# A graph attention's keys and values set up in a hand-written order, with rows and values placed through DRAM

## The chip, the cores and the metric

The kernel runs on one core of a Trainium2 chip. A core has a matrix engine (TensorE, PE in the profile), three engines for elementwise work (VectorE or DVE, ScalarE or ACT, GpSimd or POOL), and a queue engine (SyncE, SP) that issues transfers between DRAM and the on-chip memory. Each engine works through its own instructions in order; they meet only at semaphores. The metric is the device time of one execution in microseconds. Before the change it was 3151.98 us, the median of three runs (3148.44 to 3156.79).

## The reference

Two layers run one after the other on `x` of shape (4, 1024, 512), with a condition vector per batch. The first is a graph attention over 20 neighbours in two directions, the second a conditioned transformer block.

```python
row_zero = v.sum(-1) == 0
vcq = concatenate([v, where(row_zero[..., None], 0.0, q[:, None, :])], -1)
self_feat = vcq @ W_self.T + b_self
output = self_feat
for d in range(2):                       # A: the mask, or its transpose
    kv = self_feat[:, :20]
    qh = (self_feat @ Wq[d].T + bq[d])   # 16 heads of 32
    kh = (kv @ Wk[d].T + bk[d])
    aff = einsum('bnhd,bmhd->bnhm', qh, kh) / sqrt(32)
    w = softmax(where(A.sum(-1) > 0, aff, NEG) + (A @ w_bias + b_bias))
    out_t = einsum('bnhm,bmf->bnhf', w, kv)
    output += einsum('bnhf,hgf->bnhg', out_t, Wout[d]) + bout[d]
x = v + relu(output)
# then: layer norm with scale and shift from the condition, attention with
# 16 heads of 64, gated residual, and an MLP of 2048 with gelu, gated residual
```

Only the first 20 rows of a batch are keys and values in the graph attention. So 80 rows (4 batches of 20) settle everything that depends on keys and values, and that is computed once, ahead of the 32 row blocks.

## The kernel before, in words

The kernel has a set-up (lines 149 to 341), a loop over 32 blocks of 128 rows for the graph attention (lines 841 to 889), the transformer attention, and the MLP. The change touches the set-up and the start of the loop.

The set-up loads the 80 neighbour rows beside their conditions (`vcq`, lines 157 to 160), the two halves of the self weights (`wx`, `wq_in`, line 163), the biases as rows (`rows`, line 172), and per direction d the key, query and output weights (line 177). All loads are issued by SP. Then it computes, in the order of the code:

- the biases transposed to columns (`vecs`, line 187), and the condition transposed (`condT`, `scT`, line 197);
- the condition's share of the self feature, four rows (`pq`, line 203), which one matrix product per batch spreads to all 128 partitions (`pr`, line 210) and a copy puts into `qrB`;
- the self features of the 80 rows, transposed (`pf`, lines 223 to 239): 32 small products, 80 columns wide;
- per direction: keys (`pk`, line 272), values (`pvr`, line 283), the keys laid out block by block (`kbd`, line 300), and the query weights and biases folded into them (`pw`, `pb`, lines 313 and 322), copied into `kp` and `qbB` by ScalarE and VectorE in turn (`evac`, lines 78 to 83);
- the values placed so that each head's rows meet only their own 32 columns (`vb`): matrix products with a zero-one matrix `spr` (line 334) and a multiplication with a mask `own` (line 341). GpSimd builds both (lines 243 to 263).

A planner in the framework orders these instructions on each engine. From line 608 on the order is by hand: each engine issues what the code issues, in the code's order.

The loop runs steps s from -4 to 33. Step s handles several blocks at different stages: it loads block s + 4, transposes block s + 3, multiplies block s + 2 by the self weights, and so on. `g_load(i)` (line 613) issues the 128 rows of block i (`xs`, seven buffers) and two pieces of its adjacency (`a`, two buffers) on SP. An adjacency buffer comes free when GpSimd has converted it (`af`, line 675). Step -4 loads blocks 0 to 4:

```python
        for s in range(-4, NTA + 2):
            if s == -4:
                for i in range(5):
                    g_load(i)
            else:
                do(g_load, s + 4)
```

Steps -3 to 0 load blocks 1 to 4 a second time, and what later reads block 1 reads that second copy (36 loads of `xs` are in the profile for 32 blocks). The buffers of the loop lie where the set-up's tiles lay, so each waits until the tiles below it have been read for the last time.

Of the kernel before, what the change touches and what calls it, by code (L numbers as in the profile page):

```python
# [12 lines left out]
F32 = mybir.dt.float32  # L13
# [6 lines left out]
P = 128  # L20
# [21 lines left out]
def cond_block_kernel(  # L42
# [42 lines left out]

    cst = ctx.enter_context(tc.tile_pool(name="cst", bufs=1))
# [41 lines left out]
    x1d = [tc.dram_tile([P, F], F32, name=f"x1d{i}") for i in range(NTA)]  # L128
    x2d = [tc.dram_tile([P, F], F32, name=f"x2d{i}") for i in range(NTA)]


    with ExitStack() as gctx:
# [15 lines left out]

        with ExitStack() as sctx:
            sp = sctx.enter_context(tc.tile_pool(name="sp", bufs=1))  # L150
            sps = sctx.enter_context(tc.tile_pool(name="sps", bufs=4, space=PSUM))
            mps = sctx.enter_context(tc.tile_pool(name="mps", bufs=2, space=PSUM))
# [3 lines left out]
            nc.sync.dma_start(cnd, cond)  # L156
            for b in range(B):
                q = slice(b * NG, (b + 1) * NG)
                nc.sync.dma_start(vcq[q, :F], x[b * S : b * S + NG, :])
                nc.sync.dma_start(vcq[q, F:], cond[b : b + 1, :].broadcast_to([NG, F]))  # L160
            wq_in = sp.tile([P, FC, F], F32, name="wq_in")
            for t, src in ((wx, w_selfT[:F]), (wq_in, w_selfT[F:])):
                nc.sync.dma_start(t, src.rearrange("(c p) f -> p c f", p=P))
# [9 lines left out]
            ws = []  # L173
            for d in range(2):
                for src in (gwkT, gwq, gwoT):
                    t = sp.tile([P, FC, F], F32, name=f"w{d}", tag=f"w{len(ws)}")
                    nc.sync.dma_start(t, src[d].rearrange("(c p) f -> p c f", p=P))
                    ws.append(t)
            gboB = sp.tile([KV, 2, F], F32, name="gboB")
            for d in range(2):  # L180
                nc.sync.dma_start(gboB[:, d, :], gbo[d : d + 1, :].broadcast_to([KV, F]))
            nc.sync.dma_start(bsB, row(b_self).broadcast_to([P, F]))
# [3 lines left out]
            pv = sps.tile([P, F], F32, name="pv", tag="s")  # L186
            nc.tensor.transpose(pv[:, :N_VEC], rows, ident[:N_VEC, :N_VEC])
            nc.vector.tensor_copy(vecs, pv[:, :N_VEC])

            silu = sp.tile([B, F], F32, name="silu")  # L190
            nc.scalar.activation(silu, cnd, AF.Silu)
            condT = sp.tile([P, FC, B], F32, name="condT")
            nc.vector.memset(scT, 0.0)
            for t, src in ((condT, cnd), (scT[:, :, :B], silu)):
                pc = sps.tile([P, FC, B], F32, name="pc", tag="s")
                for c in range(FC):
                    nc.tensor.transpose(pc[:, c, :], src[:, c * P : (c + 1) * P], ident[:B, :B])
                nc.vector.tensor_copy(t, pc)

# [7 lines left out]
            nc.vector.tensor_copy(qrows, pq[:B])  # L207
            for b in range(B):
                pr = sps.tile([P, F], F32, name="pr", tag="s")
                nc.tensor.matmul(pr, lhsT=one_hot(0, b), rhs=qrows, start=True, stop=True)  # L210
                evac(b, qrB[:, b, :], pr)


            nz = sp.tile([KV, 1], F32, name="nz")
            nc.vector.tensor_reduce(nz, vcq[:, :F], axis=AX.X, op=ALU.add)
            nc.vector.tensor_scalar(nz, nz, 0.0, None, ALU.not_equal)
            nc.vector.tensor_scalar(vcq[:, F:], vcq[:, F:], nz, None, ALU.mult)
            vcqT = sp.tile([P, 2 * FC, KV], F32, name="vcqT")
            for h in range(2):
                pt = sps.tile([P, FC, P], F32, name="pt", tag="s")  # L220
                for c in range(FC):
                    k = h * FC + c
                    nc.tensor.transpose(pt[:, c, :KV], vcq[:, k * P : (k + 1) * P], ident[:KV, :KV])
                evac(h, vcqT[:, h * FC : (h + 1) * FC, :], pt[:, :, :KV])
            sfT = sp.tile([P, FC, KV], F32, name="sfT")
            for c in range(FC):
                pf = sps.tile([P, F], F32, name="pf", tag="s")
                for k in range(2 * FC):
                    w = wx if k < FC else wq_in
                    nc.tensor.matmul(  # L230
                        pf[:, :KV],
                        lhsT=w[:, k % FC, c * P : (c + 1) * P],
                        rhs=vcqT[:, k, :],
                        start=(k == 0),
                        stop=(k == 2 * FC - 1),
                    )
                nc.vector.tensor_scalar(
                    sfT[:, c, :], pf[:, :KV], vecs[:, V_SELF + c : V_SELF + c + 1], None, ALU.add
                )


            spr = sp.tile([KV, B, 2, GH, 2, NG], F32, name="spr")
            nc.gpsimd.memset(spr, 0.0)
            for b in range(B):
                for d in range(2):
                    nc.gpsimd.tensor_copy(
                        spr[:, b, d, :, d, :],
                        ident[:KV, b * NG : (b + 1) * NG].unsqueeze(1).to_broadcast([KV, GH, NG]),
                    )
            own = sp.tile([P, KC0, GHC, GD], F32, name="own")  # L250
            nc.gpsimd.memset(own, 1.0)
            W2 = 2 * NG
            skip = P - (GHC - 1) * W2
            for at, sign in ((0, 1), (W2 - 1, -1)):
                nc.gpsimd.affine_select(
                    out=own,
                    in_=own,
                    compare_op=ALU.is_ge,
                    fill=0.0,
                    base=at,  # L260
                    pattern=[[sign * skip, KC0], [-sign * W2, GHC], [0, GD]],
                    channel_multiplier=sign,
                )

            vrow = []
            for d in range(2):
                wk, wq, wo = ws[3 * d : 3 * d + 3]

                pk = sps.tile([P, GCH, KV], F32, name="pk", tag="s")
                for c in range(GCH):  # L270
                    for k in range(FC):
                        nc.tensor.matmul(
                            pk[:, c, :],
                            lhsT=wk[:, k, c * P : (c + 1) * P],
                            rhs=sfT[:, k, :],
                            start=(k == 0),
                            stop=(k == FC - 1),
                        )


                po = sps.tile([P, F], F32, name="pvr", tag="s")
                for k in range(FC):
                    nc.tensor.matmul(
                        po[:KV], lhsT=sfT[:, k, :], rhs=wo[:, k, :], start=(k == 0), stop=(k == FC - 1)
                    )
                v = sp.tile([KV, F], F32, name="vrow", tag="vrow", bufs=2)
                nc.vector.tensor_tensor(v, po[:KV], gboB[:, d, :], ALU.add)
                vrow.append(v)
# [7 lines left out]
                kbd = sp.tile([P, GCH, B, GHC, NG], F32, name="kbd", tag="kbd", bufs=2)  # L296
                nc.gpsimd.memset(kbd, 0.0)
                for h in range(GHC):
                    q = slice(GD * h, GD * (h + 1))
                    nc.vector.tensor_copy(  # L300
                        kbd[q, :, :, h, :], kh[q].rearrange("p c (b m) -> p c b m", b=B)
                    )

                def placed(t, c):

                    return t.rearrange("p b (h d m) -> p b h d m", d=2, m=NG)[:, :, c * GHC : (c + 1) * GHC, d, :]


                for c in range(GCH):
                    flat = kbd[:, c].rearrange("p b h m -> p (b h m)")  # L310
                    for f in range(FC):
                        pw = sps.tile([P, B, GHC, NG], F32, name="pw", tag="s")
                        nc.tensor.matmul(
                            pw.rearrange("p b h m -> p (b h m)"),
                            lhsT=wq[:, c, f * P : (f + 1) * P],
# [4 lines left out]
                        evac(f, placed(kp[:, :, f, :], c), pw)  # L320
                    pb = sps.tile([P, B, GHC, NG], F32, name="pb", tag="s")
                    nc.tensor.matmul(
                        pb.rearrange("p b h m -> p (b h m)"),
                        lhsT=vecs[:, V_Q + d * FC + c : V_Q + d * FC + c + 1].to_broadcast([P, P]),
                        rhs=flat,
                        start=True,
                        stop=True,
                    )
                    evac(c, placed(qbB, c), pb)
            for b in range(B):  # L330
                pv2 = mps.tile([P, KC0, P], F32, name="pv2", tag="m")
                for k in range(KC0):
                    for d in range(2):
# [1213 lines left out]
```

## Time and profile before

| what | value |
|---|---|
| median of three runs | 3151.98 us |
| the profiled execution | 3151.38 us, span 3149.7 us |
| TensorE busy | 3087.7 us, 98% of the span |
| set-up, last product of line 334 | ends at 88.5 us |
| first transposes of the loop (block 0) | 89.47 us |
| transposes of block 1 | 90.83 us |
| DMA in the first 30 us | 8 weight tiles of 1 MB and the small loads |

The profile is of one execution. Times in it are microseconds from the start of the span. An engine's busy time is the time in which it executes instructions; register, semaphore and DMA-issuing instructions do not count. A line of the timeline gives the start, the duration, the engine (SPq is SP's queue), the source line, the operation, the tile written and the tiles read, and in brackets the idle time before it with what ended it. A line with x8 merges eight instructions. A line of the stretches gives the stretch, its length, the busy time of PE, weight loads, DVE, ACT and POOL with instruction counts, the clock granted to TensorE as a share of full speed, the DMA share and GB/s. A line of the waits names who waited for whom, the total, the number of waits and the longest.

### The profile page before, as it was taken

The page shows a single profiled execution, that of the slowest core. Times are in us where ns is not written, and L with a number is a line of the kernel's source. Part 1 is how long each engine was busy: PE and PEld are TensorE (multiplying, and loading weights), DVE is VectorE, ACT ScalarE, POOL GpSimd, SP SyncE. Part 2 cuts the span into 40 slices and gives each one's busy share as a digit, 9 for nine tenths or more (in the row PEclk, how much of TensorE's full clock was granted, in tenths as well). Part 3 has the DMA queues.
Part 4 walks back from the last instruction along what each step waited for, and adds up shares of the span by engine and source line. Part 5 has one row for each costly group of instructions (what it writes and reads, how often), then busy time and mean ns, then how long its engine had stood idle before and what let it go on. Part 6 is the DMA issues. An engine that isn't in the chain of part 4 may idle for free.

```text
span 3149.7 us, 41147 instructions
## 1 busy us (share of the span) xinstructions
PE 3087.7 (98%) x15211; PEld 1957.9 (62%) x15211; DVE 1996.0 (63%) x2793; ACT 1437.6 (46%) x2387; POOL 1203.0 (38%) x739
## 2 busy tenths in 40 slices
PE   8999999999999999999999999999989999999999
PEld 5666665554554555454555455455458888888888
DVE  2688867777787777778777778777764232223322
ACT  1344446555665555665555665556631221112211
POOL 1344436554554654454644454555522100111010
PEclk8999999999999999999999999999999999999999
DMA  4233317776777876777776777776861010101010
GB/s 166 71 97 105 106 48 177 181 170 150 194 169 175 196 172 153 192 170 177 196 168 156 187 174 178 184 176 150 195 172 65 30 36 32 41 14 40 27 41 14
DMA packets 272859, 405.40 MB, mean 129 GB/s; under 512 B 24660, under 2 KB 97424, under 8 KB 272660
## 3 DMA queue, kind: packets, MB, share of 16 engines
q1 hardware_dynamic: 272660, 402.78, 50.8%
q8 instruction: 121, 1.98, 0.3%
q14 instruction: 78, 0.64, 0.1%
HBM read 109.08 MB, written 25.17 MB: 43 GB/s over the span
## 4 chain that ended last, share of the span: by engine, by line
PE 85%; DVE 5%; ACT 3%; issue 2%; DMA 2%; SPq 1%; POOL 1%; POOLq 0%; DVEq 0%; ACTq 0%
PE q L467 16%; PE psc L1065 14%; PE pav L1027 13%; PE pout L1045 7%; PE mbd L467 5%; PE mbu L467 5%; PE mad L467 4%; PE mau L467 3%; PE pa L695 2%; PE mcd L467 2%; PE pf L655 2%; ACT w L1082 2%; PE mdd L467 2%; PE mdu L467 2%; PE mcu L467 2%
## 5 line engine op out<-in xcount | busy, mean ns | idle before, releaser
L1091 POOL TENSOR_SCALAR w<-w,sm 128x1024 f32<-128x1024 f32 x256 | 733.8, 2866 | 884.3 <-DVE sm L1087 884.1
L1082 ACT ACTIVATE w<-psc,mx 128x1024 f32<-128x1024 f32 x512 | 570.5, 1114 | 645.3 <-DVE mx L1076 644.5
L1100 DVE STREAM_TRANSPOSE wd<-w 128x1024 f32<-128x1024 f32 x512 | 633.8, 1238 | 134.8 <-ACT w L1089 115.1
L1076 DVE TENSOR_REDUCE mx<-psc 128x1 f32<-128x1024 f32 x512 | 599.5, 1211 | 102.5 <-PE psc L1065 99.8
L1065 PE MATMUL psc<-kT,qT 64*128 64x512 f32 x2048 | 531.3, 617 | 6.8 <-ACT w L1082 4.2
L1027 PE MATMUL pav<-wT,v 128*64 128x256 f32 x4096 | 475.1, 382 | 2.3 <-DMA wT<-wd 1.7
L1027 PEld LDWEIGHTS pav<-wT,v 128*64 128x64 f32 x4096 | 290.1, 137 | 225.3 <-issue 70.4
L1065 PEld LDWEIGHTS psc<-kT,qT 64*128 64x128 f32 x2048 | 204.2, 186 | 262.7 <-issue 158.0
L1089 ACT ACTIVATE w<-w,sm 128x1024 f32<-128x1024 f32 x256 | 291.0, 1137 | 0.0
L1045 PE MATMUL pout<-wout,oT 128*128 128x512 f32 x512 | 243.5, 609 | 5.8 <-DVE xr L1053 5.8
L449 POOL TENSOR_TENSOR tx<-hT 128x512 f32<-128x512 f32 x8 | 10.2, 1270 | 568.5 <-DVE hT L388 568.5
L467 PE MATMUL q<-hT,wqk 128*128 128x512 f32 (+1 forms) x396 | 183.1, 586 | 6.7 <-DVE q L481 6.7
L1045 PEld LDWEIGHTS pout<-wout,oT 128*128 128x128 f32 x512 | 92.9, 191 | 137.4 <-issue 118.0
L489 ACT COPY mbu<-mau 128x512 f32<-128x512 f32 x30 | 17.1, 570 | 291.7 <-PE mau L467 291.7
L695 PE MATMUL pa<-kp,sfT 128*128 128x320 f32 x512 | 143.5, 433 | 1.4 <-ACT sfT L670 1.4
L1053 DVE TENSOR_TENSOR xr<-pout,xr 128x512 f32<-128x512 f32 x128 | 85.5, 680 | 85.4 <-PE pout L1045 85.1
L467 PEld LDWEIGHTS q<-hT,wqk 128*128 128x128 f32 x396 | 73.1, 190 | 102.7 <-issue 99.1
L467 PE MATMUL q<-tx,ex 128*128 128x512 f32 (+1 forms) x264 | 126.6, 603 | 0.0
L695 PEld LDWEIGHTS pa<-kp,sfT 128*128 128x128 f32 x512 | 94.8, 190 | 38.2 <-ACT sfT L670 1.9
L655 PE MATMUL pf<-wx,xT 128*128 128x512 f32 x256 | 115.3, 593 | 0.3 <-DVE pf L637 0.3
L467 PE MATMUL mad<-w,hs 128*128 128x256 f32 x512 | 113.1, 379 | 0.0
L467 PEld LDWEIGHTS mad<-w,hs 128*128 128x128 f32 x512 | 97.3, 190 | 13.2
(303 smaller groups left out, 4364.8 us busy)
## 6 DMA issues: line engine op xcount, KB each, us to landing
wT<-wd SPq DMA_DIRECT2D x1024, 256.0 KB
wqk<-in_w_qkv SPq DMA_DIRECT2D x64, 256.0 KB
xs<-in_x SPq DMA_DIRECT2D x36, 256.0 KB
x1d<-xs SPq DMA_DIRECT2D x32, 256.0 KB
xl<-x1d SPq DMA_DIRECT2D x32, 256.0 KB
wv<-in_w_qkv SPq DMA_DIRECT2D x32, 256.0 KB
xr<-x1d SPq DMA_DIRECT2D x32, 256.0 KB
wout<-in_w_out SPq DMA_DIRECT2D x16, 512.0 KB
```

The source lines that it names most:

```text
L467: nc.tensor.matmul(t[:, q * width : (q + 1) * width], lhsT=lhs(which, q, k), rhs=rhs(which, q, k), start=(fresh and q == 0 and k == 0), st ...
L655: nc.tensor.matmul(pfs[i], lhsT=xT[i][:, c, :], rhs=wx[:, c, :], start=False, stop=(c == FC - 1), skip_group_check=True,)
L695: nc.tensor.matmul(pas[i][:, n, :HF], lhsT=sfT2[i][:, c, :], rhs=kp[:, b, c, n * HF : (n + 1) * HF], start=False, stop=(c == FC - 1), skip ...
L1027: nc.tensor.matmul(po[j * D : (j + 1) * D, :], lhsT=vt[b, g][:, m, p * P + j * D : p * P + (j + 1) * D], rhs=w[:, j, :, m, :], start=(m == 0),
L1045: nc.tensor.matmul(po, lhsT=oT[b, 2 * g + p][:, n * P : (n + 1) * P], rhs=wout[b, g][:, p, :], start=(p == 0), stop=(p == 1),)
L1053: nc.vector.tensor_tensor(t, po, t, ALU.add)
L1065: nc.tensor.matmul(sc[j][:, n * F : (n + 1) * F], lhsT=qT[b, gp][q, t * P : (t + 1) * P], rhs=kT[b, gp][q, n * F : (n + 1) * F], start=Tru ...
L1076: nc.vector.tensor_reduce(mx, sc, axis=AX.X, op=ALU.max, negate=True)
L1082: nc.scalar.activation(w, sc, AF.Exp, bias=mx, accum_out=sm)
L1089: nc.scalar.mul(w, w, sm)
L1091: nc.gpsimd.tensor_scalar(w, w, sm, None, ALU.mult)
L1100: nc.vector.transpose(wd[j][:, :, at, :], wn.pop((b, gp, t, j)).rearrange("p (m k) -> p m k", k=U))
```

## The change

- The order by hand begins at the top of the kernel, so it covers the set-up too.
- Until the first loads land, TensorE multiplies a cleared tile `warm` by itself, seven products of 512 columns.
- The neighbour rows and the condition are loaded on ScalarE's queue, the weights on SP's. The self weights' first half comes first, and per direction the order is key, output, query weights. A direction's row bias follows its weights.
- The buffers of `xs` and `a` move to a pool of their own, opened ahead of the set-up, and blocks 0 and 1 are loaded right behind the weights. Step -4 loads blocks 2 to 4. The second loads of blocks 1 to 4 stay.
- The self features are summed in one bank, first over the rows' half of the weights for all four column chunks, then over the condition's half, with the small transposes between. The bias rows are transposed after that.
- The four condition rows are written to DRAM and read back onto all partitions, in place of the products `pr`.
- The values are written to DRAM and read back head by head into a cleared `vb`: 36 small loads on SP (16 heads, two directions, four heads cut in two at a multiple of 128 rows). The products of line 334, `spr` and `own` are gone.
- The order of the rest is keys 0, values 0, keys 1, folding 0, values 1, folding 1. Half of the copies into `kbd` go to ScalarE. The set-up has seven PSUM banks for its tiles in place of four, and one for the busy work.

```diff
+    ctx.enter_context(tc.manual_schedule())
     cst = ctx.enter_context(tc.tile_pool(name="cst", bufs=1))
...
+    qrd = tc.dram_tile([B, F], F32, name="qrd")
+    vrd = [tc.dram_tile([KV, F], F32, name=f"vrd{d}") for d in range(2)]
...
+        lp = gctx.enter_context(tc.tile_pool(name="lp", bufs=1, reuse_waits="tile"))
+        def g_load(i):
+            xs[i] = lp.tile([P, F], F32, name="xs", tag="xs", bufs=7)
+            nc.sync.dma_start(xs[i], x[i * P : (i + 1) * P, :])
+            adjs[i] = lp.tile([P, 2, NG * NL], I32, name="a", tag="a", bufs=2)
+            for d in range(2):
+                nc.sync.dma_start(adjs[i][:, d, :], adj[d, i * P : (i + 1) * P, :])
...
-            sps = sctx.enter_context(tc.tile_pool(name="sps", bufs=4, space=PSUM))
-            mps = sctx.enter_context(tc.tile_pool(name="mps", bufs=2, space=PSUM))
+            sps = sctx.enter_context(tc.tile_pool(name="sps", bufs=7, space=PSUM))
+            wps = sctx.enter_context(tc.tile_pool(name="wps", bufs=1, space=PSUM))
...
+                nc.scalar.dma_start(vcq[b * NG : (b + 1) * NG, :F], x[b * S : b * S + NG, :])
+            nc.sync.dma_start(wx, w_selfT[:F].rearrange("(c p) f -> p c f", p=P))
+            nc.scalar.dma_start(cnd, cond)
+            for b in range(B):
+                nc.scalar.dma_start(
+                    vcq[b * NG : (b + 1) * NG, F:], cond[b : b + 1, :].broadcast_to([NG, F])
+                )
+            nc.sync.dma_start(wq_in, w_selfT[F:].rearrange("(c p) f -> p c f", p=P))
...
+                for k, src in ((0, gwkT), (2, gwoT), (1, gwq)):
+                    nc.sync.dma_start(ws[3 * d + k], src[d].rearrange("(c p) f -> p c f", p=P))
                 nc.sync.dma_start(gboB[:, d, :], gbo[d : d + 1, :].broadcast_to([KV, F]))
+            for i in range(2):
+                g_load(i)
...
+            warm = sp.tile([P, F], F32, name="warm")
+            nc.vector.memset(warm, 0.0)
+            for d in range(2):
+                nc.gpsimd.memset(kbds[d], 0.0)
+            nc.gpsimd.memset(vb, 0.0)
+            def warming(n):
+                t = wps.tile([P, F], F32, name="pwarm", tag="warm")
+                for _ in range(n):
+                    nc.tensor.matmul(t, lhsT=warm[:, :P], rhs=warm, start=True, stop=True)
+            warming(7)
...
+            neighbours(0)
+            nc.vector.tensor_scalar(vcq[:, F:], vcq[:, F:], nz, None, ALU.mult)
+            through_self(0)
+            neighbours(1)
...
+            through_self(1)
...
-                pr = sps.tile([P, F], F32, name="pr", tag="s")
-                nc.tensor.matmul(pr, lhsT=one_hot(0, b), rhs=qrows, start=True, stop=True)
-                evac(b, qrB[:, b, :], pr)
+            nc.scalar.copy(qrows, pq[:B])
+            nc.sync.dma_start(qrd, qrows)
+                nc.sync.dma_start(qrB[:, b, :], qrd[b : b + 1, :].broadcast_to([P, F]))
...
+                nc.vector.tensor_tensor(v, po[:KV], gboB[:, d, :], ALU.add)
+                nc.sync.dma_start(vrd[d], v)
+
+            def spread_values(d):
+                src = vrd[d].rearrange("(b m) f -> m b f", b=B)
+                for h in range(GH):
+                    q = (2 * h + d) * NG
+                    cuts = [q, *range((q // P + 1) * P, q + NG, P), q + NG]
+                    for a, z in zip(cuts, cuts[1:]):
+                        k, p = divmod(a, P)
+                        col = h * GD - k * 3 * GD
+                        nc.sync.dma_start(
+                            vb[p : p + z - a, :, k, col : col + GD],
+                            src[a - q : z - q, :, h * GD : (h + 1) * GD],
+                        )
...
+            keys(0)
+            values(0)
+            keys(1)
+            spread_values(0)
+            folded(0)
+            values(1)
+            spread_values(1)
+            folded(1)
...
-        ctx.enter_context(tc.manual_schedule())
...
-                for i in range(5):
+                for i in range(2, 5):
                     g_load(i)
```

## The prediction

> **What bounds the kernel now.** I read the page's head first, then the chain that ended last, then the opening by tens of microseconds, then its timeline, then the load queue's own waits.
>
> ```profile
> span 3149.7 us, 41147 instructions
> ...
> PE 3087.7 (98%) x15211; PEld 1957.9 (62%) x15211; DVE 1996.0 (63%) x2793; ACT 1437.6 (46%) x2387; POOL 1203.0 (38%) x739
> ...
> PE 85%; DVE 5%; ACT 3%; issue 2%; DMA 2%; SPq 1%; POOL 1%; POOLq 0%; DVEq 0%; ACTq 0%
> ```
>
> TensorE is busy 98% of the span and carries 85% of the chain. What shortens its opening shortens the kernel, as long as nothing late makes it wait. The opening, in the answer by stretches (its last columns: granted clock, DMA share, GB/s):
>
> ```profile
> 10.00:20.00 10.00, 7.07 (x17) 1.92 (x17) 0.57 (x3) 0.00 (x0) 3.43 (x4) 1.00 1.05 403
> 20.00:30.00 10.00, 9.23 (x27) 5.05 (x27) 2.55 (x4) 1.60 (x3) 0.00 (x0) 0.63 1.03 372
> 30.00:40.00 10.00, 10.00 (x49) 10.00 (x49) 0.90 (x3) 0.00 (x0) 0.00 (x0) 0.50 0.02 4
> 2340.00:2350.00 10.00, 4.23 (x7) 1.57 (x6) 8.11 (x21) 0.00 (x0) 0.00 (x0) 0.68 0.50 155
> ```
>
> From 22.5 to 46.4 us TensorE is busy but granted half its clock, while the loads are over by 30. The last line shows what a gap costs: TensorE idles 5.77 us there. The timeline:
>
> ```profile
> 12.94 0.33 PE L187 MATMUL pv<-ident,rows 60*128 60x60 f32 x1 [12.94 <-DMA rows<-in_b_mod]
> ...
> 14.13 6.06 PE L203 MATMUL pq<-wq_in,condT 128*4 128x512 f32 x8
> ...
> 20.96 5.67 PE L210 MATMUL pr<-qrows,ident 4*128 4x512 f32 x8 [0.77 <-DVE qrows L207]
> ...
> 27.88 2.00 PE L230 MATMUL pf<-vcqT,wx 128*128 128x80 f32 x8
> ...
> 61.68 3.69 PE L272 MATMUL pk<-sfT,w 128*128 128x80 f32 x32
> ...
> 79.42 9.10 PE L334 MATMUL pv<-vrow,spr 80*128 80x128 f32 x80
> ...
> 90.83 0.66 PE L649 MATMUL pt<-ident,xs 128*128 128x128 f32 x4
> ```
>
> TensorE starts at 12.94, when the bias rows land behind the weights. The pr and the 80-product pv go with the change, pq and pf should run faster. The last line, the transposes of row block 1, is my mark: everything after 90.83 is the same work in the same order, so its new time gives the result. The load queue:
>
> ```profile
> SPq L618 <- POOL af L675: 47.4, 4, 21.9
> ...
> 61.95 0.80 SPq L618 DMA_DIRECT2D a<-in_adj  x2
> 62.80 0.43 SPq L615 DMA_DIRECT2D xs<-in_x  x1
> 63.33 0.85 SPq L618 DMA_DIRECT2D a<-in_adj  x2
> ```
>
> Row blocks are loaded in order on SP and waiting there costs nothing today: what block 1 needs is issued at 65.65, 25 us early. That cover is what the change uses up.
>
> **The change part by part.** Every matrix product here is two TensorE instructions. A half of 512 columns takes 0.43 us at full clock, 0.86 at half (the pq row's spacing); an 80-column half 0.110 (32 from 61.84 to 65.38 on the chain) or 0.213 (64 from 27.9 to 41.5).
>
> *Keeping TensorE busy.* Seven products of zeros, 14 halves, start once VectorE has cleared their 512 columns, near 1.6. The clock came up 5.1 us after pq's dense halves began (spacing falls at about 19.2) and 3.8 us after work resumed at 2346.65. So they end between 1.6 + 3.8 + 9.6 x 0.43 = 9.5 and 10.2; if zeros do not count, at 1.6 + 12.0 = 13.6. I take 10.2. Loads: neighbour rows were used 1.5 us after issue and go first now; the two self weights need 2 MB at the 409 GB/s shown, 5.1 us, and land by 9. Nine loads on ScalarE's own queue at 0.33 us take 3 us of an engine idle until 22 today; its first copy is due at 10.7. GpSimd's clearings (2.3 us, and 2.2 for the values by half of the 4.36 us memset) end by 7 and are due at 27: nothing.
>
> A rule against the whole idea: the Trainium skill, TensorE: Matmul & The Clock Gate, "Why this matters for your kernels", asks for 4 us of continuous work and no more for full clock. Here TensorE was busy 15 us (27.9 to 42.8) in 80-column products and stayed at 0.50. By the page the self stage would run at full clock after the warm-up and the price below would be 0, not 2.5.
>
> *Self stage.* From 10.2: four transposes and ScalarE's copy 1.1 (0.5 + 0.43 + hand-over); 32 halves 3.5; four transposes, eight small ones for the condition, a copy: 1.6; 32 halves 3.5; biases 0.3; pq 3.4. That is 23.6. At half clock the second 32 cost 3.3 more and pq 1.7 more, 5.0. The 1.6 us of thin work in the middle may drop the clock: it fell at 22.5 after an interval with pq to 20.2 and four-row products behind it, yet stayed up through 80-column products mixed with dense ones (60 to 65). I take half of the range 0 to 5.0: 2.5, so 26.1.
>
> *Keys and values.* keys 3.5, values 3.4, keys 3.5, folding four times 2.69 (the chain's 2.15 + 0.54): 10.8; values 3.4. Call the end of those second values E: 26.1 + 24.6 = 50.7. The second folding ends at E + 10.8. The four-row spreading of the query rows (5.7 us) and the 80 spreading products (9.1 us) are gone from TensorE; the DRAM trips replacing them are on SP. VectorE's one add for the self stage (320 columns, 0.49 as kh) lies beside pq. Copies keep up: 0.43 and 0.49 us on two engines against 0.54 per fold. Then 0.95 idle and 1.4 to the mark, as in 88.51 to 90.83: E + 13.1 = 63.8 if block 1 is there.
>
> *What is late next.* SP now holds, in order: query rows out (about 26), four reads back, values 0 out, 18 small loads, values 1 out, 18 small loads, and only then blocks 2, 3, 4 and block 1 again (line 846 repeats it, and the transposes read the repeat). The first set (values 0 end at 33.0, the same steps as below) is through by about 44, before E. The second: VectorE's add and issue E + 1.35; the write lands about 1.9 later. No row shows a write to DRAM awaited; a small load took 1.2 (condition, 1.17 to 2.36), a loaded queue 3.0 (64.18 to 67.16); 1.9 is nearer the first because the queue is empty. Then 18 issues. Twenty-row loads of vcq are issued every 0.37 us, wb and bb every 0.64; four loads into interleaved columns of wm took 2.08, so interleaving forces no wait. I take 0.41: 7.4. SP is free at E + 10.6. Before, from the first a at 61.95, a of block 4 landed at 68.6 by the wait of its successor; block 1's rows, behind it in the queue, 0.8 later (256 KB at the 330 GB/s between the last two landings): 7.4 after 61.95, plus 0.8 for block 2's rows, now in front: 8.2. Unloaded bound: 4.55 + 1.2 = 5.8. So block 1 is there at E + 18.8, and TensorE waits 5.7 (2.6 at the best ends, 10 with 0.64).
>
> The Trainium skill, DMA: Bandwidth & Descriptors, "Specifications", wants 512 B per piece for line rate; these are 128 B. Priced as 512 B, an estimate, 1,440 pieces are 0.74 MB, 1.8 us at 409 GB/s, under the 7.4 of issuing, so its sum is mine; no row here shows 128-byte pieces.
>
> *The gap's clock.* After the 5.77 us gap the clock was back 3.8 us after resuming: 1.9 us lost. I add 1.9.
>
> **Sum:** 63.8 + 5.7 + 1.9 = 71.4 against 90.83: 19.4 us less. The profiled execution took 3151.4 (its span and 1.7 around it); 3132.0. The median of the three runs is 0.6 higher: 3132.6.
>
> **The rivals.**
> *No late block.* The small loads issue at 0.37 and block 1 lands unloaded; stall at most 2.6, no clock loss, and the self stage stays warm: E 48.2, mark 63.9, 26.9 less, 3125. For: DMA is idle then. Against: 65.65 to about 69.4 for the same load before.
> *The busy work has no effect.* Zeros do not raise the clock. Warm-up ends 13.6; the self stage costs 1.3 + 6.8 + 2.2 + 6.8 + 0.3 + 5.1; E is 60.7, mark 81.4, 9.4 less, 3143. For: the four-row products at 20.96 did not hold the clock, so not all work counts. Against: these use all 128 rows.
> *Slower: SP serialises the small loads.* If each waits for the one before (2.2 us), the first set, from 36.3, ends near 76, the second near 118, block 1 comes at 126, and with 1.9 of clock the mark is 37 us later: 3189. It decides from 1.2 us per load (36.3 + 36 x 1.17 + 2.25 + 8.2 + 1.9 = 90.8). Against: vcq's and wm's paces of 0.37 and 0.52 into one tile.
> *Dearer issue*, 0.64: 4.1 more, 3137, inside the main case's range.
>
> **How the numbers follow.** Main case with dearer issue 0.65, no late block 0.12, no effect 0.14, serialised 0.09. Measurement tells about 0.3% (9.5 us; the runs spread over 3148.4 to 3156.8). Faster: 0.65 + 0.12 + half of 0.14, less a few hundredths for dear issue with a cold self stage: 0.81; same 0.11; slower 0.08. Range: from 3124 (no late block) to 3146 (no effect, with a dearer issue's 4 us); the main case's own is 3127 to 3140.
>
> **What would show it.** The mark near 71; a TensorE wait of 3 to 10 us just before it, put down to the load of xs; the clock at 0.50 for a few microseconds after it; pw starting near 36 instead of 50.9; 36 small loads about 0.4 us apart on SP. I am wrong if the self stage's products take 0.21 us throughout, if the small loads lie over 1.2 us apart, or if the wait before the mark is absent.

## The result, and the profile after

The changed kernel takes 3132.76 us, the median of four runs (3130.72 to 3134.16), against 3150.21 us for the kernel before on the same chip (four runs, 3148.18 to 3156.79). The ratio is 0.9945, with a 95% interval from 0.9928 to 0.9961: 17.5 us less. The prediction was 3132.6. The profiled execution took 3134.16 us, its span 3132.4.

The head of the page of the changed kernel, and the line of its chain by engines:

```profile
span 3132.4 us, 41033 instructions
...
PE 3074.0 (98%) x15137; PEld 1939.2 (62%) x15137; DVE 1989.6 (64%) x2780; ACT 1440.3 (46%) x2391; POOL 1195.1 (38%) x728
...
PE 84%; DVE 5%; ACT 4%; DMA 2%; issue 2%; SPq 2%; POOL 1%; POOLq 0%; DVEq 0%; ACTq 0%
```

TensorE is still busy 98% of the span. It has 13.7 us less of busy time, and SP's queue holds 2% of the chain in place of 1%. Its timeline through the opening:

```profile
1.47 9.27 PE L215 MATMUL pwarm<-warm 128*128 128x512 f32 x14 [1.47 <-DVE warm L205]
10.57 0.44 PE L230 MATMUL pt<-ident,vcq 80*128 80x80 f32 x4
11.53 3.80 PE L237 MATMUL pf<-vcqT,wx 128*128 128x80 f32 x32 [0.52 <-ACT vcqT L81]
...
16.19 3.80 PE L237 MATMUL pf<-vcqT,wq_in 128*128 128x80 f32 x32
...
20.11 3.60 PE L270 MATMUL pq<-wq_in,condT 128*4 128x512 f32 x8
23.64 3.80 PE L284 MATMUL pk<-sfT,w 128*128 128x80 f32 x32
...
34.24 2.36 PE L343 MATMUL pw<-kbd,w 128*128 128x320 f32 x8
...
45.05 3.60 PE L308 MATMUL pvr<-w,sfT 128*80 128x512 f32 x8
...
60.05 0.63 PE L663 MATMUL pt<-ident,xs 128*128 128x128 f32 x4 [0.63 <-issue]
...
68.90 1.08 PE L663 MATMUL pt<-ident,xs 128*128 128x128 f32 x4 [7.37 <-DMA xs<-in_x]
```

The zeros run to 10.6. The self stage's products take 3.80 per 32 halves (1.91 per 8 before), `pq` 3.60 in place of 6.06. The second values end at 48.5, the second folding at 59.4. Block 0 is transposed at once, block 1 only at 68.90: 7.37 us of idle TensorE, put down to the load of its rows. That is the mark; it stood at 90.83 before, so 21.9 us earlier. The stretches (granted clock in the third column from the end):

```profile
10.00:20.00 10.00, 9.48 (x83) 8.64 (x81) 1.23 (x4) 2.34 (x3) 0.00 (x0) 1.00 0.69 224
20.00:30.00 10.00, 10.00 (x48) 5.35 (x49) 1.84 (x5) 1.49 (x3) 0.00 (x0) 1.00 1.05 374
30.00:40.00 10.00, 10.00 (x57) 7.82 (x56) 3.91 (x9) 2.94 (x7) 1.60 (x2) 1.00 0.69 211
...
66.00:70.00 4.00, 1.10 (x5) 1.13 (x6) 0.15 (x1) 0.72 (x2) 0.42 (x1) 0.50 0.92 265
70.00:74.00 4.00, 4.00 (x7) 1.56 (x7) 0.00 (x0) 0.59 (x1) 1.18 (x2) 0.70 0.77 225
```

The half clock from 22.5 to 46.4 us is gone: the stretch from 30 to 40 is granted 1.00 in place of 0.50. A short one has come behind the wait: 0.50 in the last line but one, and 0.70 over the four microseconds after it, so it lasted until about 72.4, 3.5 us beyond the restart, and cost about 1.8. The load queue's timeline, SP alone:

```profile
33.90 0.33 SPq L199 DMA_DIRECT2D bsB<-in_b_self  x1
...
35.51 0.28 SPq L275 DMA_DIRECT2D qrd<-qrows  x1
38.19 1.75 SPq L277 DMA_DIRECT2D qrB<-qrd  x4
40.04 0.37 SPq L317 DMA_DIRECT2D vrd<-vrow  x1
44.45 6.67 SPq L327 DMA_DIRECT2D vb<-vrd  x18
51.22 0.32 SPq L317 DMA_DIRECT2D vrd<-vrow  x1
53.21 6.66 SPq L327 DMA_DIRECT2D vb<-vrd  x18
59.91 0.36 SPq L157 DMA_DIRECT2D xs<-in_x  x1
...
65.01 0.43 SPq L157 DMA_DIRECT2D xs<-in_x  x1
```

The 36 small loads go out 0.37 us apart, and behind them, at 65.01, the repeated load of block 1. Its rows were in the chip already (lines 157 and 160 issue blocks 0 and 1 from 23.00 us on); the repeat fills another buffer, and that is the one the transposes read.

The mark is one instruction, and half clock after it gives some of its gain back. So the experiments are also read at the first scores product of the transformer attention (`psc`), by which all of this is settled. A line of this view gives the number of instructions, the shortest, median and longest in ns, and the first and last start. Before, and changed:

```profile
L1065 PE MATMUL psc<-kT,qT x2048: 589/589/1057, 456.9 to 2308.8; 64*128 64x512 f32 x187
```

```profile
L1079 PE MATMUL psc<-kT,qT x2048: 589/589/1219, 436.1 to 2289.1; 64*128 64x512 f32 x187
```

That is 20.8 less. The span is only 17.3 less. Of the other 3.5, the half-clock stretches in the later stages are 2.3; they vary from execution to execution (last section). The last 1.2 are open.

### The profile page after: what moved, and what is told of

The parts are those of the page before. It is cut to its first block, busy times and chain, and to the rows that moved or that the text cites. A ratio compares the mean times of both kernels' runs of the same rounds, so it can differ in the third digit from the quotient of the medians.

```text
span 3132.4 us, 41033 instructions
## 1 busy us (share of the span) xinstructions
PE 3074.0 (98%) x15137; PEld 1939.2 (62%) x15137; DVE 1989.6 (64%) x2780; ACT 1440.3 (46%) x2391; POOL 1195.1 (38%) x728
## 4 chain that ended last, share of the span: by engine, by line
PE 84%; DVE 5%; ACT 4%; DMA 2%; issue 2%; SPq 2%; POOL 1%; POOLq 0%; DVEq 0%; ACTq 0%
PE q L489 16%; PE psc L1079 14%; PE pav L1041 13%; PE pout L1059 7%; PE mbd L489 5%; PE mbu L489 5%; PE mad L489 4%; PE mau L489 3%; PE pa L709 2%; ACT w L1096 2%; PE mcd L489 2%; PE pf L669 2%; PE mdd L489 2%; PE mcu L489 2%; PE mdu L489 2%
```

## The experiments

Theory: TensorE's opening is shorter because the zeros bring the clock up and the four-row and spreading products are gone; the end of the opening is then set by block 1's repeated load, late because SP issues it behind the 36 small loads. Rivals: the wait has another cause (DMA traffic, buffers); the zeros do nothing and the gain is the order alone; the trips through DRAM cost nothing. All microseconds; "lost" is what half clock took after `psc`, the sum over stretches of 25 us of (1 - granted clock) x length.

| kernel | mark | first `psc` | `psc` to end | lost |
|---|---|---|---|---|
| before | 90.83 | 456.9 | 2692.8 | 16.1 |
| changed | 68.90 | 436.1 | 2696.3 | 18.4 |
| changed, second profile | 69.28 | 436.2 | 2685.5 | 9.4 |
| changed, no repeated loads | 61.39 | 427.4 | 2691.0 | 11.3 |
| changed, no small loads of direction 1 | 61.42 | 427.5 | 2683.8 | 5.8 |
| changed, no zeros | 74.08 | 440.9 | 2688.9 | 12.9 |
| changed, one load queue | 67.28 | 434.8 | 2699.9 | 21.5 |
| changed, rows by products | 75.94 | 443.0 | 2689.0 | 10.9 |
| changed, values by products | 70.27 | 436.4 | 2689.4 | 10.8 |
| before, no repeated loads | 91.34 | 457.4 | 2694.2 | 16.5 |
| before, zeros ahead | 85.07 | 451.1 | 2696.7 | 18.4 |
| no repeat, seven products of zeros | 60.05 | 426.1 | 2689.6 | 14.7 |
| no repeat, five | 67.26 | 433.3 | 2689.0 | 12.9 |
| no repeat, five, second profile | 59.41 | 425.4 | 2689.5 | 12.5 |

### The changed kernel without the repeated loads

```diff
-            else:
+            elif s > 0:
                 do(g_load, s + 4)
```

> The changed kernel without the second loads of blocks 1 to 4; the first copies are read instead. Theory (TensorE's 7.4 us wait at 61.5 is for the repeated load of block 1, queued on SP behind the small value loads): the transposes of block 1 start at 61.4 instead of 68.9, the clock stays at 1.00 there, and the first product of the transformer attention's scores moves from 436.1 to 426.9: 9.2 us less (7.4 of waiting and 1.85 of half clock). Rival (SP is simply late for everything, the wait moves to block 2): the scores come only 2 to 4 us earlier, with a new wait before the transposes of block 2.

Mark 61.39, no wait before it. TensorE's timeline:

```profile
60.04 0.63 PE L663 MATMUL pt<-ident,xs 128*128 128x128 f32 x4 [0.63 <-issue]
...
61.39 0.66 PE L663 MATMUL pt<-ident,xs 128*128 128x128 f32 x4
```

The two transposes stand 1.35 us apart, as before the change. The first `psc` comes 8.6 us earlier than in the changed kernel: the 7.4 of the wait and 1.2 of the 1.8 of the clock. The repeat was the wait.

### The changed kernel without the small loads of direction 1

This leaves direction 1's values out: `vb` holds zeros for that direction. Everything that TensorE does is issued as before.

```diff
             values(1)
-            spread_values(1)
             folded(1)
```

> The changed kernel without the 18 small loads of the second direction's values: that direction's values are left at zero, so part of the computation is left out. The repeated loads stay. Theory (the small loads are what makes the repeat late): SP reaches block 2 at about 51.7 instead of 59.9, block 1's repeat lands at about 60.7, the transposes of block 1 start at 61.4, and the first scores product comes at 426.9 as without the repeats. Rival (the repeat itself is slow, whatever is ahead of it): a wait of 3 us or more is left, scores at 430 or later.

The repeat stays, only the 18 small loads ahead of it are gone. SP's timeline:

```profile
50.15 0.32 SPq L317 DMA_DIRECT2D vrd<-vrow  x1
50.51 0.42 SPq L157 DMA_DIRECT2D xs<-in_x  x1
```

SP goes from the write of the values straight to block 2's rows, 9.4 us earlier, and the mark is at 61.42 without a wait. So the repeat by itself costs nothing; it costs because of what stands ahead of it on SP, and taking away half of the 36 small loads was enough. For SP's queue and against the traffic speak also the five executions that wait: the mark follows SP's arrival at block 2's rows by 8.4 to 9.2 us in each (59.91 and 68.90 in the changed kernel, 65.36 and 74.08 without the zeros). Together the two runs show both halves of the theory.

### The kernel before without the repeated loads

The same edit in the kernel before.

> The kernel before without the second loads of blocks 1 to 4. Theory (there the repeated load was 20 us early, so it cost nothing): the transposes of block 1 start at 90.8 and the first scores product at 456.9, each within 0.5 us. Rival (the repeats cost DMA or queue time in both kernels): 2 us or more less.

Mark 91.34, first `psc` 457.4: 0.5 later, and TensorE also began 0.4 later (13.33 for 12.94). The repeats were free before. The change made them dear.

### The changed kernel without the zeros

```diff
-            warming(7)
```

> The changed kernel without the seven products of zeros. Theory (they raise the clock, and that is all they do): TensorE begins at about 9.2 when the neighbour rows land, the clock is low through the self stage, whose 80-column halves take 0.213 us instead of 0.110, and comes up in pq; the second values end at 56.6 instead of 48.5; SP's small loads shift by about 6, so the transposes of block 1 start at 75.1 instead of 68.9: 6.2 us more. Rival 1 (the loads set the pace): at most 1 us more. Rival 2 (SP's own queue sets the start of block 1 at 59.9 + 9 whatever TensorE does): 0 to 1 us more, with a shorter wait before it.

TensorE begins at 8.43, and the self stage runs at half speed:

```profile
18.23 7.12 PE L236 MATMUL pf<-vcqT,wq_in 128*128 128x80 f32 x32
...
25.57 5.41 PE L269 MATMUL pq<-wq_in,condT 128*4 128x512 f32 x8
...
74.08 1.09 PE L662 MATMUL pt<-ident,xs 128*128 128x128 f32 x4 [5.28 <-DMA xs<-in_x]
```

7.12 us for 32 halves in place of 3.80. The second values end at 55.8 in place of 48.5, 7.3 later. The mark comes only 5.2 later (6.2 were expected): SP, which reached the second values' write late in the changed kernel, now stands waiting for them and issues it at 56.67 in place of 51.22, 5.5 later. So the wait for block 1 shrinks by 2.1, and `psc` comes 4.9 later. The zeros do raise the clock, and they are worth about 4.9 us.

### The changed kernel with the four rows spread by products

```diff
             nc.scalar.copy(qrows, pq[:B])
-            nc.sync.dma_start(qrd, qrows)
             for b in range(B):
-                nc.sync.dma_start(qrB[:, b, :], qrd[b : b + 1, :].broadcast_to([P, F]))
+                pr = sps.tile([P, F], F32, name="pr", tag="s")
+                nc.tensor.matmul(pr, lhsT=one_hot(0, b), rhs=qrows, start=True, stop=True)
+                evac(b, qrB[:, b, :], pr)
```

> The changed kernel with the four condition rows spread by products again (pr), in place of the trip through DRAM. pr costs 3.4 us at full clock; SP is relieved of one write and four reads. Theory (products that use four rows of the array don't hold the clock up): the clock falls within 4 us of pr, the keys run at 0.213 us a half, and the transposes of block 1 start near 74.6 instead of 68.9. Rival (any product holds the clock): the second values end 3.4 later at full clock, the transposes of block 1 at 70.6.

`psc` 443.0, 6.9 later, although the zeros ended 1.5 us sooner in this execution (9.03 for 10.57); like for like the loss is nearer 8.5. The timeline behind `pq`:

```profile
22.84 5.18 PE L277 MATMUL pr<-qrows,ident 4*128 4x512 f32 x8 [0.67 <-ACT qrows L274]
27.95 7.11 PE L285 MATMUL pk<-sfT,w 128*128 128x80 f32 x32
34.85 5.44 PE L309 MATMUL pvr<-w,sfT 128*80 128x512 f32 x8
```

The four-row products do not hold the clock. It falls at about 25, inside `pr`; the first keys take 7.11 in place of 3.80, and it is back in the middle of the first values. Of the pieces undone here, their DRAM trip is worth most, and more for the clock (3.3 us of the keys and 1.8 of the values) than for their own time. TensorE also idled 0.67 us ahead of `pr`; that this is not needed for the fall shows in the kernel before with zeros, below.

### The changed kernel with the values spread by products

The spreading matrices are built by GpSimd, as before the change, in buffers that the weights have left; the set-up's PSUM banks are split as before (four, and two tiles for these products). The edit without these two:

```diff
...
-                nc.sync.dma_start(vrd[d], v)
+                vrow.append(v)
...
-            spread_values(0)
...
-            spread_values(1)
             folded(1)
+            for b in range(B):
+                pv2 = mps.tile([P, KC0, P], F32, name="pv2", tag="m")
+                for k in range(KC0):
+                    for d in range(2):
+                        nc.tensor.matmul(
+                            pv2[:, k, :],
+                            lhsT=sprs[b][:, d].rearrange("p h d m -> p (h d m)")[:, k * P : (k + 1) * P],
+                            rhs=vrow[d][:, k * 3 * GD : k * 3 * GD + P],
+                            start=(d == 0),
+                            stop=(d == 1),
+                        )
+                nc.vector.tensor_tensor(vb[:, b], pv2, own.rearrange("p k h j -> p k (h j)"), ALU.mult)
```

> The changed kernel with the values placed by the 80 products and the mask of before, in place of the DRAM trips; all else stays, the repeated loads too. Theory (the DRAM trips took 9 us off TensorE and gave it back as the wait and the half clock): folding ends at 59.3, the products take 9.0, the transposes of block 1 start near 70.7 without a wait and at full clock, and the first scores product comes at 436 as with the DRAM trips, within 1.5 us. Rival (the trips are a gain of 9 us): scores at 444 to 446.

```profile
58.87 9.10 PE L395 MATMUL pv<-vrow,spr 80*128 80x128 f32 x80
68.93 0.63 PE L702 MATMUL pt<-ident,xs 128*128 128x128 f32 x4 [0.96 <-issue]
...
70.27 0.66 PE L702 MATMUL pt<-ident,xs 128*128 128x128 f32 x4
```

`psc` at 436.4 against 436.1, with zeros that ended 0.95 us sooner (9.62 for 10.57), so like for like the trip is worth some 1.2 us. The 9.1 us of products fill the time in which the changed kernel waits, and with the small loads gone from SP nothing waits. In this change the values' trip through DRAM bought next to nothing; what it took from TensorE came back as the wait and its clock loss. Without the repeated loads the trip is worth the difference between 436.4 and 427.4, and that 0.95 more.

### The changed kernel with one load queue

The nine loads of the neighbour rows and the condition are issued by SP, in the same place (`nc.sync.dma_start` for `nc.scalar.dma_start`).

> The changed kernel with all loads on SP, in the same order. Theory (the second queue lets the neighbour rows and the self weights share the engines and delays SP's later weights, whose issue waits for these rows to land): the weights from gwkT on are issued at about 7.2 instead of 12.0, SP is free for the first value write 4 us earlier, the second value write goes at 49.6 instead of 51.2, and the transposes of block 1 start at 67.3 instead of 68.9: 1.6 us less. Rival (two queues bring the first data sooner, which is the bound): the self stage begins 1.5 to 3 us later and so does the mark.

Mark 67.28 (67.3 was expected), `psc` 1.3 earlier than with two queues. About 0.5 of that is the zeros' end (10.04 for 10.57), which varies; the rest is SP, which issues the first values' write at 37.44 in place of 40.04. The second queue brings nothing here. One reason shows in the waits of SP in the changed kernel:

```profile
SPq L189 <- DMA vcq<-in_x: 6.6, 2, 5.0
...
SPq L189 <- DMA wq_in<-in_w_selfT: 2.0, 1, 2.0
```

SP, at the bias rows, waits for landings of `vcq`, which the other queue issued. So the first key weights went out at 12.01, where one queue issued them at 9.44, and everything behind them on SP was later. And the neighbour rows, issued from 0.71 on by a queue of their own, are late too: without the zeros TensorE began with them at 8.43, waiting for that load. They were on their way beside 2 MB of weights.

### The kernel before with nine products of zeros ahead

```diff
+            warm = sp.tile([P, F], F32, name="warm")
+            nc.vector.memset(warm, 0.0)
+            pwarm = sps.tile([P, F], F32, name="pwarm", tag="s")
+            for _ in range(9):
+                nc.tensor.matmul(pwarm, lhsT=warm[:, :P], rhs=warm, start=True, stop=True)
```

> The kernel before with nine products of zeros ahead of the set-up, everything else as it was. Theory (the clock falls again in the four-row products pr at 21 to 26): pq runs at 0.43 us a half, 2.6 us earlier in all, the self stage still runs at half clock, and the first scores product comes at 454.3 instead of 456.9. Rival (once up, the clock stays up through the set-up): pq 2.6, pr 2.2, the self stage 6.6 and the first keys 2 less: scores near 443.

`psc` at 451.1, 5.8 earlier, between the two expectations. TensorE's timeline:

```profile
13.90 3.60 PE L209 MATMUL pq<-wq_in,condT 128*4 128x512 f32 x8
18.27 3.69 PE L216 MATMUL pr<-qrows,ident 4*128 4x512 f32 x8 [0.77 <-DVE qrows L213]
...
22.91 2.00 PE L236 MATMUL pf<-vcqT,wx 128*128 128x80 f32 x8 [0.24 <-ACT vcqT L81]
```

`pq` and even `pr` run at full clock now, but the clock falls at about 22.7, behind them, and the self stage stands at half speed again. TensorE had been busy without a break from 18.27 to 22.67, with `pr` and then 0.8 us of transposes; so no idle time is needed for the fall. The theory's mechanism held, and its size missed what `pr` gained by starting warm. Zeros alone are not the change: the four rows had to go too.

### The changed kernel again, and without the repeat with five products of zeros

In the changed kernel the neighbour rows are there at about 8.5 and the zeros end at 10.6; five products should end nearer.

```diff
-            warming(7)
+            warming(5)
...
-            else:
+            elif s > 0:
                 do(g_load, s + 4)
```

> The changed kernel as it is, timed beside the one above on the same chip. Transposes of block 1 at 68.9, first scores product at 436.1; 3132, within 4 us, of which the part after the scores (2690 to 2700 so far) is moved only by half-clock stretches there.

> The changed kernel without the second loads of blocks 1 to 4, and with five products of zeros in place of seven. Theory (the zeros are needed until the clock is up, and the data is there at about 8.5): TensorE passes to the neighbour rows at 8.8 to 10.0 instead of 10.6, the self stage still runs at full clock, the transposes of block 1 start at 59.6 to 60.8, the first scores product comes near 426.3, and the time is 3122 (about 0.991 of before, 10 us less than the changed kernel). Rival (five do not hold the clock until the self stage): the self stage falls to 0.213 us a half and the first scores product comes at 430 or later.

The changed kernel took 3127.79 us here (six runs, 3123.50 to 3131.47; ratio to the kernel before 0.9932, 0.9914 to 0.9950), its wait before the mark 7.73; 3132 within 4 was expected, so it is just outside. The variant took 3117.55 us (six runs, 3111.38 to 3127.61; ratio 0.9901, 0.9880 to 0.9922). But its profiled execution had lost the clock. The same kernel was run again beside the seven:

> The same with five products of zeros, beside the one with seven. Theory (with five TensorE idles about 1 us before the neighbour rows, and the 80-column products do not keep the clock up after such a gap): the self stage is at half clock again for most of its length, first scores product near 433, time some 3 to 6 us above the kernel with seven. Rival (it was the chance of one execution): self stage at full clock, first scores product at 426.3, time 1 us below the kernel with seven.

3117.92 us (six runs, 3112.14 to 3123.48; ratio 0.9899, 0.9881 to 0.9917), and this time the profile is at full speed: the rival's case, the chance of one execution. The same stretch of the two executions of the same kernel, first and second:

```profile
12.00:16.00 4.00, 4.00 (x24) 3.83 (x24) 0.49 (x1) 0.00 (x0) 0.00 (x0) 0.50 0.79 230
```

```profile
12.00:16.00 4.00, 4.00 (x41) 3.83 (x40) 0.75 (x3) 0.00 (x0) 0.00 (x0) 1.00 0.82 258
```

24 products at 0.50 against 41 at 1.00, with `psc` at 433.3 against 425.4. With five, TensorE idles for 0.97 and 0.90 us behind the zeros until the neighbour rows are there.

### Without the repeat, with seven

> The changed kernel without the second loads of blocks 1 to 4, seven products of zeros, timed. Theory (the wait and the half clock behind it are gone for good): block 1 at 61.4, self stage at full clock, first scores product at 427.4 less or more 1.5; about 9 us under the changed kernel, 0.990 of before. Rival (the earlier single time of 3120 was luck of the clock in the later stages): 3 us or less under the changed kernel.

3118.45 us (six runs, 3117.45 to 3125.34; ratio 0.9906, 0.9887 to 0.9925). With seven products there is no idle time behind the zeros, and the self stage ran at full clock in each of the eight profiled executions that have them. Five and seven can't be told apart by time here; whether five lose the clock often is open. All three of these results lie below both kernels. The edit of one line, no repeated loads, brings some 8 to 9 us on top of the change (8.2 by the ratios, 3118.45 for 3127.79 by the medians). The intervals of the two ratios overlap, but the first `psc` leaves no doubt: 426.1 for 436.2, of which 1.4 is the zeros' end (9.22 for 10.58).

The early loads of blocks 0 and 1, the new order of the set-up and the additional PSUM banks were not undone alone.

## Why the prediction was right

**Keeping TensorE busy.** Taken: zeros until 10.2, and they count. Measured 10.6, and they count.

**Self stage.** Taken 26.1, of which 2.5 was half of an allowance for a falling clock. The stage ended at 23.64, the all-warm sum of 23.6; that it fits to the tenth is luck, since the zeros ended 0.4 later and the stage itself took 0.3 less. The thin work in its middle (1.0 us of transposes and small products) never dropped the clock. The term that was mis-sized is this 2.5: it measured 0. The rule weighed there, the Trainium skill's TensorE: Matmul & The Clock Gate, "Why this matters for your kernels", that 4 us of continuous work bring full clock, would have priced it at 0 and been right on the price. It is not right on the reason: without the zeros, the same 80-column products ran 7.12 us without a break at half speed.

**Keys and values.** Taken 24.6 from there to the end of the second values, measured 24.8; from there to the mark without a wait 13.1, and 12.9 in the run without repeats.

**What is late next.** The mechanism was right as written: SP's small loads, and behind them the repeat of block 1. Its terms were off in both directions. The waits of SP in the changed kernel:

```profile
SPq L327 <- DMA vrd<-vrow: 5.6, 2, 4.0
...
SPq L199 <- DMA w<-in_gwq: 2.8, 1, 2.8
...
SPq L277 <- DMA qrd<-qrows: 2.3, 1, 2.3
```

A small load took 0.37, not 0.41 (-0.7 in all). The first set was to be through by 44 and was through at 51.1. The second values were ready about 49.4 (0.9 behind their products, as from 47.96 to 48.87 in the run with one queue) and waited 1.8 for SP to write them. That step failed: it let the first set start as soon as the first values were there, whose products ended at 30.7, but SP stood at the bias loads until 33.90, behind the weights' landings, and then at the query rows' trip until 39.9; and the first values' write, behind 1 MB of `qrB`, took 4.0 to land, where 1.9 was taken. The second took 1.7. (The prediction said that no row shows a write to DRAM awaited; the kernel before has one, 1.9 us for the last write of `out`.) The load of block 1 came 9.0 after SP was free, not 8.2. In all 20.4 behind the second values, where 18.8 was taken, and the wait was 7.4, not 5.7.

**The gap's clock.** Taken 1.9, measured about 1.8.

So -2.5 and +1.7 nearly met: mark 68.90 for 69.5 (the sum's 71.4, and with it the "mark near 71", holds the 1.9 of clock that come behind the mark). At `psc` the kernel had gained 20.8, where 19.4 was predicted; the later stages, 3.5 longer in that execution, left 17.3. By the medians the gain is 17.5, and the kernel before stood 1.8 lower in its four runs (3150.21) than in the three from which the forecast started (3151.98). So the hit to 0.2 us is luck: a gain 1.9 too high, from a start 1.8 too high. The terms of the sum are right to 2.5.

**The rivals.** No late block: excluded by the 7.37. No effect of the zeros: excluded by the run without them. Serialised small loads, 1.2 us apart or more: they were 0.37 apart. The other rule, the Trainium skill's DMA: Bandwidth & Descriptors, "Specifications", with its 512 B for line rate, did not bear: 18 loads of 128-byte pieces (1,280 pieces, not the 1,440 of the prediction) went out in 6.67 us, issued one by one, and their sum was that of the issues.

**What the prediction did not price.** It took the second queue as costing nothing. The run with one queue shows 0.7 to 1.3 us against it, from one execution.

## What to carry to other kernels

Work that is taken from the bounding engine is a gain only when what comes next in line is ready sooner as well; list, per queue, what the new transfers are put in front of, down to a load that looked free (here a repeated one, worth 9 us once 36 small loads stood ahead of it). Bring the clock up with wide products on all rows, and leave no four-row products and as little idle time as can be between them and the real work. And judge an opening of some tens of microseconds at a mark behind it, not by the total: the rest of this kernel varies by as much.

## What the runs showed of the hardware that was not expected

**What raises the clock and what only keeps it.** Starting from half clock, 80-column products did not raise it: 15 us in the kernel before, 7.12 us without the zeros, 7.11 us behind `pr`. Each time it came up only after the next 512-column halves on all rows had begun, but not after a fixed time: 3.5 us in the kernel before (42.90 to 46.42), 3.7 without the zeros, inside `pq`, and 3.7 behind `pr`, inside the values; 1.9 in the kernel before with zeros (37.92 to 39.81), 4.7 with the five products that lost it (23.66 to 28.37). Once the clock was up, the same 80-column products kept it (11.53 to 20 in the changed kernel). With the four-row `pr` it fell each time, inside the products or within 1 us behind them. That the width is the cause, or the four rows, and not what goes with them, was not tried alone.

**The granted clock is not to be trusted in the first microseconds.** Without the zeros, this stretch falls in products that take 0.213 us each in place of 0.110:

```profile
12.00:16.00 4.00, 4.00 (x21) 4.00 (x20) 0.00 (x0) 0.00 (x0) 0.00 (x0) 1.00 0.75 250
```

The column says 1.00, with 21 products, where a stretch at full speed has 41 and one at 0.50 has 21 to 24. Until the first recorded change, read the products' own durations.

**The later stages vary mostly with the clock.** From `psc` to the end the profiled executions took 2683.8 to 2699.9 us. Less what half clock took, they took 2674.9 to 2679.7, whatever the kernel: 16 us of scatter become 5. The same work, 20 us apart because of the opening, in the changed kernel and then in the kernel before:

```profile
2562.00:2594.00 32.00, 31.28 (x132) 25.05 (x131) 7.72 (x11) 4.51 (x10) 9.87 (x8) 0.89 0.11 33
```

```profile
2582.00:2614.00 32.00, 31.28 (x147) 26.11 (x146) 8.42 (x12) 3.74 (x8) 9.88 (x8) 1.00 0.10 34
```

The same busy time, with 15 products fewer and a clock of 0.89: a dip that one execution has and the other does not. In the kernel before the clock fell at 22.53 and rose at 46.42, 23.89 us apart, and two later dips, at 466.26 and 2343.59, lasted 6.83 each. These are 7 and 2 times 3.413. In the fourteen traces all 174 stretches between two changes of the granted clock are whole multiples of 3.413 us, to 0.01. The Trainium skill, TensorE: Matmul & The Clock Gate, Part 1, states a free-running window of 3.413 us for the clock's decision; these rows agree. Such a window would make it chance whether a gap of 0.9 us loses the clock; that the two executions with five products differ by it is argued, not shown.

**The zeros' end varies too.** The same 14 halves took from 7.73 to 9.29 us in the executions with seven products, by where in them the clock rose: at 4.42 and at 7.57 in the shortest and the longest.
